# Laying rotated queries in DRAM once and reading them twice over, with a new order around the first sequence's stacks

## The chip, the core and the metric

The kernel runs on one core of one Trainium2 chip. The metric is the device time of one execution in microseconds (us). All engine names are those of the profile: PE is TensorE with PEld for its weight loads, DVE is VectorE, ACT is ScalarE, POOL is GpSimd, SP is SyncE. SP computes nothing here; it issues nearly all DMAs, one after the other, in the order in which the program lists them ("SPq" in the profile). 16 DMA engines move the data.

## What is computed

For each of 8 sequences x of 512 tokens and 256 features:

```
xn = layernorm(x)
q, k, v = xn @ in_proj_w.T, 16 heads of 16 features; q and k rotated (rope)
s = softmax(q k' / 4, keys j with 0 <= t - j < 250) v, then @ out_proj_w.T
h = relu([xn, -xn] @ +-1 weights) -> 1024; relu(h @ +-1 weights) -> 1024; -> 256
out = x + s * silu(h)
```

Everything is fp32. The +-1 weight matrices come as booleans.

## The kernel before, in words

**Splitting numbers in two.** A matmul reads its fp32 operands with fewer bits than they have. So q and k are split into a high part (hi) and a low part (lo), and a score is built as hi·hi + lo·lo + hi·lo + lo·hi. One head has 8 feature pairs x 2 places in the pair = 16 rows; the four products make 64 rows of contraction, and two heads fill 128 partitions. Such a 128-row operand is called a stack. A stack of k and one of q serve a pair of heads; a group g is four heads, so it has two pairs and needs four stacks. There are four groups in a sequence.

**How a stack is made.** `project` (L371) computes one half of q or k for all heads on PE into PSUM, DVE multiplies it with the rope tables (L397), `rotate` (L414) adds on POOL. `split_hi` (L431) rounds the high part on ACT into the tile `hi` and calls `to_dram`; `split_lo` (L437) subtracts on DVE and calls `to_dram` for the low part. `to_dram` (L420) writes each part to DRAM twice, by two DMAs of 512 KB: for k in the order hi, lo, hi, lo in a head's rows, for q in the order hi, lo, lo, hi, so that all four products meet when the 64 rows are contracted. `stack` (L444) then reads, for each pair and for k and q, 128 rows of 512 numbers (256 KB) from consecutive DRAM rows into an SBUF tile: four DMAs for a group, each out of the double-buffered pool `stacks` (bufs=2 for each of k0, q0, k1, q1).

**Attention.** A sequence has six steps (L702 to L721). `scores` (L735) does 12 matmuls for a step: first four of pair 0, then four of pair 1 (both with y = 0), then two each. Group 0 is used in steps 0 and 1, group 1 in 1 and 2, group 2 in 3 and 4, group 3 in 4 and 5. `exponentials` (L756) runs ACT over the score banks, `mask` (L781) clears on POOL, and the step after that multiplies with the values (`values`, L810). When a group is done, `keep` (L839) copies the PSUM bank `po` twice: for even groups into V (times a 0/1 column) and S by ACT, for odd groups by DVE.

**The order of the work.** `run` (L234) sorts pieces by a planner's time, in units in which one sequence takes 42, and emits them; each engine executes its instructions in that order. A piece may return followers with a delay; `project` gives `rotate`, `split_hi` (after `hi_after`) and `split_lo` (after `lo_after`), counted in the same units. `attention` (L869) places the steps among the matmuls of the feed-forward network and places the stack reads: in the first sequence (b = 0) groups 0 and 1 are read together at planner time 24.7 - 7.6 = 17.1; in later sequences group 0 is read before the sequence starts and group 1 just after it has started. The layernorm moments of sequence 1 go through DRAM as well: `lay_down` (L283) at 16.9 transposes on DVE and issues four small DMAs (L289), `load_xT` (L279) at 17.15 loads x transposed, and `lay_over` (L291) at 17.2 reads the moments back, spread over all partitions, in one DMA (L298, tile `of_all`). DVE then normalizes (L309), and PE projects k (L381, tile `ka_ps`).

**Division.** Sums of exponentials go through DRAM: `gather` (L913, tile `dsums`, DMAs of four rows), `pack` (L922, `sums`), `invert` (L929, `inv`), `unpack` (L942, `rows`). All are issued by SP, in line with the stack reads. Each next DMA of the chain waits on SP until the one before it has landed.

Of the kernel before, what the change touches and what calls it, by code (L numbers as in the profile page):

```python
# [11 lines left out]
F32 = mybir.dt.float32  # L12
# [4 lines left out]
ALU = mybir.AluOpType  # L17
# [17 lines left out]
def tile_attention_times_gated_ffn(  # L35
# [42 lines left out]
    nc = tc.nc  # L78
    P = 128
    B, T, E = x.shape  # L80
    H = HEADS
    D = E // H
# [19 lines left out]
    dram = ctx.enter_context(tc.tile_pool(name="dram", bufs=2, space=bass.MemoryType.DRAM))  # L102
# [4 lines left out]
    def bank(name):  # L107
        return ps_b.tile([P, T], F32, tag="b", name=name)
# [12 lines left out]
    first_half, second_half = s_sb[:, 3:4], s_sb[:, 4:5]  # L121
# [48 lines left out]
    rows = const.tile([P, T], F32, name="rows")  # L170
# [200 lines left out]
    def project(b, what, part, half=None):  # L371

        st = states[b]
        col = E * "qk".index(what) + P * "ab".index(part)
        if half == 1:
            ps = st.pop(part)
        else:
            ps = st[part] = bank(f"{what}{part}_ps_{b}")
        for cols in [slice(0, T)] if half is None else [ts(half, T // 2)]:
            for c in range(EC):  # L380
                nc.tensor.matmul(  # L381
                    ps[:, cols], wqkv_sb[:, c, ds(col, P)], st["xT"][:, c, cols],
                    start=(c == 0), stop=(c == EC - 1),
                )
        if half == 0:
            return

        m = turned.tile(
            [P, 2, T], F32, tag=f"m{part}", name=f"m_{what}{part}_{b}",
            bufs=2 if part == "a" else 1,  # L390
        )
        st[what, part] = m

        hi_after, lo_after = (4.0, 5.1) if b else (5.0, 6.2) if what == "k" else (4.6, 5.4)

        def times(i):
            nc.vector.tensor_tensor(  # L397
                m[:, i], ps, rope_sb[:, i if part == "a" else 1 - i], ALU.mult
            )

        def both():
            times(0)
            times(1)
            if part == "b":
                return [
                    (1.4, lambda: rotate(b, what)),
                    (hi_after, lambda: split_hi(b, what)),
                    (lo_after, lambda: split_lo(b, what)),
                ]


        return [(1.5 if b == 0 and what + part == "qb" else 0.0, both)]

    def rotate(b, what):  # L414
        st = states[b]
        m, n = st[what, "a"], st.pop((what, "b"))
        for i, op in enumerate((ALU.subtract, ALU.add)):
            nc.gpsimd.tensor_tensor(m[:, i], m[:, i], n[:, i], op)  # L418

    def to_dram(b, what, part, tile_):  # L420

        st = states[b]
        if part == 0:
            st["dram", what] = dram.tile([P, 8, T], F32, tag=what, name=f"d{what}_{b}")
        for turn in range(2):
            place = 2 * turn + (part ^ (turn if what == "q" else 0))
            nc.sync.dma_start(
                st["dram", what][:, ds(2 * place, 2), :], tile_.bitcast(F32)
            )

    def split_hi(b, what):  # L431
        st = states[b]
        hi = st["hi"] = turned.tile([P, 2, T], F32R, tag="hi", name=f"{what}h_{b}")
        nc.scalar.copy(hi, st[what, "a"])
        to_dram(b, what, 0, hi)

    def split_lo(b, what):  # L437
        st = states[b]
        m = st.pop((what, "a"))
        lo = m.bitcast(F32R)  # L440
        nc.vector.tensor_tensor(lo, m, st["hi"].bitcast(F32), ALU.subtract)
        to_dram(b, what, 1, lo)

    def stack(b, g):  # L444
        st = states[b]
        for pair in range(2):
            for what in "kq":
                t = stacks.tile([P, T], F32R, tag=f"{what}{pair}", name=f"{what}_{b}_{g}_{pair}")
                rows = st["dram", what][ds(32 * g + 16 * pair, 16)]
                nc.sync.dma_start(t.bitcast(F32), rows.rearrange("p n t -> (p n) t"))  # L450
                st[what, g, pair] = t

    def prepare(b, plain=False):
# [26 lines left out]
        for what in "kq":  # L480
            for n, part in enumerate("ab"):
                if b == 0 and what == "k" and not plain:

                    out += [
                        (-34.3 if n == 0 else -32.95, 0.87, lambda p=part: project(b, "k", p, 0)),
                        (at["k"] + dp * n, 0.87, lambda p=part: project(b, "k", p, 1)),
                    ]
                else:
                    out.append((
                        at[what] + dp * n, 1.75, lambda w=what, p=part: project(b, w, p),  # L490
                    ))
# [347 lines left out]
    def keep(b, g, po):  # L839

        st = states[b]
        odd = g % 2
        S = st["S", g] = outs.tile([P, T], F32, tag="S", name=f"S_{b}_{g}", bufs=3)
        if odd:
            V = st["V", g // 2]
            nc.vector.scalar_tensor_tensor(V, po, second_half, V, ALU.mult, ALU.add)
            nc.vector.tensor_copy(S, po)
        else:
            V = st["V", g // 2] = outs.tile(
                [P, T], F32, tag=f"V{g // 2}", name=f"V_{b}_{g}", bufs=2  # L850
            )
            nc.scalar.mul(V, po, first_half)
            nc.scalar.copy(S, po)

    def flush():
        if pending:
# [4 lines left out]
    def step(b, i):  # L861
        sc = scores(b, i)
        had = len(pending)
        more = flush() or []
        tiles, exps, rest = exponentials(b, i, sc)
        pending.append((rest, (b, i, tiles)))
        return [(-1.4 if had else 0.0, exps)] + more

    def attention(b, among):  # L869

        first, end = SEQ * b + (24.7 if b == 0 else 0.0), ends_at(b)
        inside = sorted((at, cost) for at, cost, _ in among if first <= at < end)
        whole = sum(cost for _, cost in inside)
        times, done = [], 0.0
        places = {}
        for at, cost in inside:
            if at in quick or b == 0 and at not in inner:
                places[at] = done
            done += cost
        for n in range(len(steps)):  # L880
            at = min(places, key=lambda at: abs(places[at] * len(steps) - whole * n))
            del places[at]
            times.append(at - 0.01)
        out = []
        for n in range(len(steps)):
            out.append((times[n], 2.5, lambda n=n: step(b, n)))
        for g in range(NG):

            at = times[used[g - 2][-1]] + 0.01 if g > 1 else first - (
                7.6 if b == 0 else 4.0 if b == 1 else 9.0  # L890
            )
            if b and g == 3:
                at += 5.0
            if b and g == 1:
                at = first + 0.01
            out.append((at, 0, lambda g=g: stack(b, g)))
        if b + 1 == B:
            out.append((end, 0.7, flush))
        return out

    def ends_at(b):
        return SEQ * b + (33.0 if b + 1 == B else SEQ)
# [158 lines left out]
    for b in range(B):  # L1061
# [4 lines left out]
        for t in range(NT):  # L1066
            if b + 1 < B:
                at = SEQ * b + 1.5 if b else 2.0
                everything.append((at + t, 0, lambda b=b, t=t: load_x(b + 1, t)))
        everything += divisions(b) + finish(b, b + 1 == B)  # L1070
    for b in range(B):
        everything += attention(b, everything)
# [54 lines left out]
    with tc.If(found < n_rows, label="general"):  # L1127
        for b in range(B):
            for t in range(NT):
                load_x(b, t)  # L1130
            run(prepare(b, plain=True))
            plain_ffn(b)
            for u in range(len(outputs(b))):
                run(finish_ffn(b, u, "at once"))
            for g in range(NG):
                stack(b, g)
                po = ps_o.tile([P, T], F32, tag="po", name=f"f_po_{b}_{g}")
                for t in range(NT):
                    for r in range(4):
                        shifted(b, g, t, r, po)  # L1140
                keep(b, g, po)
                if g % 2:
                    run(divisions(b, (g // 2,)))
            run(finish(b))
# [59 lines left out]
```

## Time and profile before

| | |
|---|---|
| runs | 598.86 us median of 3 (598.08 to 601.21) |
| the profiled execution | 598.20 us; its span from first to last instruction 596.5 us |
| granted TensorE clock in it | 0.999 |
| PE busy | 584.8 us, 98% of the span |
| DVE, ACT, POOL busy | 333.7, 303.0, 269.9 us |
| DMA | 92.24 MB, mean 155 GB/s; 38.30 MB written to and 53.22 MB read from DRAM (HBM) |
| queue q1 (SP's DMAs) | 47600 packets, 89.31 MB, 44.1% of the 16 engines' time |
| stack reads | 64 of k and 64 of q, 256 KB each |
| writes of q and k | 32 for each, 512 KB each |

The profile comes from one execution; 1.7 us of its time lie before its first and after its last instruction. A row of a timeline gives start and duration in us from the span's start, the engine, the source line, the operation, out<-in, and how many instructions were merged. For a DMA such a row is only the issue on SP; when the data is there is told by its landing events, of which each DMA engine that took part in a DMA sends one.

### The profile page before, as it was taken

Reading aid. Unit: us, or ns where it says so; the run is one execution under the profiler, and the core shown is the slowest. Engines: PE = TensorE matmul, PEld = TensorE weight load, DVE = VectorE, ACT = ScalarE, POOL = GpSimd, SP = SyncE. Lnnn points to the kernel's source line nnn. Section 1 sums busy time; section 2 is a strip of 40 time slices with the busy share of each in tenths; the row PEclk is TensorE's granted clock in tenths of the full one; section 3 lists DMA queues with packets and bytes.
Section 4 is the critical chain, followed back from the end, with each engine's and each line's share of the span. In section 5 each row is a group of like instructions: output and inputs, shape, how many; then the busy total and the mean of one; then the engine's idle time right before and its main releaser. Section 6 shows DMA issues by size and latency. Waiting matters only on the chain.

```text
span 596.5 us, 10410 instructions
## 1 busy us (share of the span) xinstructions
PE 584.8 (98%) x3788; PEld 364.7 (61%) x3788; DVE 333.7 (56%) x578; ACT 303.0 (51%) x571; POOL 269.9 (45%) x474
## 2 busy tenths in 40 slices
PE   7999999999999999999999999999999999999996
PEld 6655565655655556555566556665566555657785
DVE  6936335666346754478436684366744666427256
ACT  4747564545464545536454465544644645465422
POOL 2736533436334552445444355333652437435513
PEclk9999999999999999999999999999999999999999
DMA  9764844337432474415654075441673335441111
GB/s 277 283 234 143 294 152 127 108 141 250 146 117 98 170 240 133 147 65 223 208 165 154 2 293 189 130 142 65 238 228 113 107 135 208 158 143 43 35 28 53
DMA packets 50086, 92.24 MB, mean 155 GB/s; under 512 B 10992, under 2 KB 18672, under 8 KB 50032
## 3 DMA queue, kind: packets, MB, share of 16 engines
q1 hardware_dynamic: 47600, 89.31, 44.1%
q10 hardware_dynamic: 2432, 2.23, 1.2%
q8 instruction: 31, 0.51, 0.3%
q14 instruction: 23, 0.19, 0.1%
HBM read 53.22 MB, written 38.30 MB: 153 GB/s over the span
## 4 chain that ended last, share of the span: by engine, by line
PE 88%; DVE 3%; DMA 3%; ACT 2%; SPq 1%; POOL 1%; issue 1%; DVEq 0%; POOLq 0%; ACTq 0%
PE h_ps L511 44%; PE po L828 11%; PE z_ps L562 9%; PE sc L746 7%; PE v_ps L361 4%; PE att_ps L962 4%; PE ka_ps L381 2%; PE qb_ps L381 2%; PE qa_ps L381 2%; PE kb_ps L381 2%; DMA of_all<-d 1%; DMA dq<-m_qa 1%; PE warm L232 1%; SPq L450 1%; DMA dk<-kh 1%
## 5 line engine op out<-in xcount | busy, mean ns | idle before, releaser
L771 ACT ACTIVATE p<-sc 128x512 f32<-128x512 f32 (+2 forms) x288 | 150.2, 607 | 57.6 <-PE sc L746 57.4
L791 POOL TENSOR_SCALAR_AFFINE_SELECT p<-p 128x256 f32<-128x256 f32 (+1 forms) x224 | 104.8, 479 | 123.1 <-ACT p L771 105.4
L511 PE MATMUL h_ps<-h1l,w_sb 128*128 128x512 f32 (+1 forms) x576 | 145.3, 394 | 0.0
L511 PE MATMUL h_ps<-h1h,w_sb 128*128 128x512 f16 (+1 forms) x576 | 123.1, 356 | 0.0
L511 PEld LDWEIGHTS h_ps<-h1l,w_sb 128*128 128x128 f32 x576 | 100.4, 188 | 27.4 <-issue 5.7
L511 PEld LDWEIGHTS <-w_sb 128*128 128x128 f16 x704 | 61.3, 98 | 86.3 <-issue 41.5
L522 ACT ACTIVATE h2h<-h_ps 128x512 f16<-128x512 f32 (+1 forms) x72 | 39.6, 550 | 133.1 <-PE h_ps L511 133.1
L520 DVE SCALAR_TENSOR_TENSOR h2l<-h_ps,h2h 128x512 fp32r<-128x512 f32 (+1 forms) x72 | 44.8, 622 | 93.9 <-ACT h2h L522 93.4
L828 PE MATMUL po<-p,v_pad 128*32 128x378 f32 (+4 forms) x1152 | 71.5, 380 | 0.0
L520 DVE SCALAR_TENSOR_TENSOR h1l<-h_ps,h1h 128x512 fp32r<-128x512 f32 x64 | 43.2, 688 | 45.3 <-ACT h1h L522 45.1
L798 POOL TENSOR_SCALAR_AFFINE_SELECT p<-p 128x256 f32<-128x256 f32 x144 | 57.5, 399 | 0.3 <-POOL p L791 0.3
L746 PEld LDWEIGHTS sc<-q,k 64*128 64x128 f32 x576 | 41.9, 186 | 25.0 <-issue 15.1
L633 DVE RECIPROCAL den<-den 128x256 f32<-128x256 f32 (+1 forms) x32 | 52.4, 1641 | 3.7 <-ACT den L628 3.7
L746 PE MATMUL sc<-q,k 64*128 64x378 f32 (+4 forms) x576 | 52.2, 310 | 2.2 <-ACT p L771 1.2
L522 ACT ACTIVATE h1h<-h_ps 128x512 f16<-128x512 f32 x64 | 37.6, 603 | 30.0 <-PE h_ps L511 30.0
L511 PE MATMUL h_ps<-xl,w_sb 128*128 128x512 f32 x128 | 52.3, 489 | 0.0
L952 POOL TENSOR_TENSOR V<-V,R 128x512 f32<-128x512 f32 x16 | 21.2, 1327 | 52.4 <-DVE R L951 52.4
L828 PEld LDWEIGHTS po<-p,v_pad 128*32 128x32 f32 x1152 | 30.7, 109 | 21.2 <-issue 12.0
L991 POOL TENSOR_TENSOR gate<-gate,xr 128x512 f32<-128x512 f32 (+1 forms) x15 | 18.6, 1242 | 47.6 <-DVE gate L984 26.6
L418 POOL TENSOR_TENSOR m_qa<-m_qa,m_qb 128x512 f32<-128x512 f32 x16 | 21.1, 1343 | 38.5 <-DVE m_qb L397 38.5
L511 PE MATMUL h_ps<-xh,w_sb 128*128 128x512 f16 x128 | 38.5, 383 | 0.0
L562 PE MATMUL z_ps<-h2l,w_sb 128*128 128x512 f32 (+1 forms) x144 | 35.6, 389 | 0.0
(102 smaller groups left out, 656.9 us busy)
## 6 DMA issues: line engine op xcount, KB each, us to landing
k<-dk SPq DMA_DIRECT2D x64, 256.0 KB
q<-dq SPq DMA_DIRECT2D x64, 256.0 KB
dk<-kh SPq DMA_DIRECT2D x16, 512.0 KB
dk<-m_ka SPq DMA_DIRECT2D x16, 512.0 KB
dq<-qh SPq DMA_DIRECT2D x16, 512.0 KB
dq<-m_qa SPq DMA_DIRECT2D x16, 512.0 KB
x<-in_x_dram SPq DMA_DIRECT2D x30, 128.0 KB
xT<-in_x_t_dram SPq DMA_DIRECT2D x7, 512.0 KB
```

Source lines behind the costliest of these rows:

```text
L361: nc.tensor.matmul(v.rearrange("p n s d -> p (n s d)"), st["xT"][:, c, ts(t, P)], wqkv_sb[:, c, 2 * E :], start=(c == 0), stop=(c == EC - 1),)
L381: nc.tensor.matmul(ps[:, cols], wqkv_sb[:, c, ds(col, P)], st["xT"][:, c, cols], start=(c == 0), stop=(c == EC - 1),)
L511: nc.tensor.matmul(ph, weights(w, p, c, ts(f, P)), st[src + p][:, c, cols], start=(k == 0), stop=(k == n - 1),)
L520: nc.vector.scalar_tensor_tensor(lo, ph, 0.0, hi, ALU.max, ALU.subtract)
L522: high = lambda: nc.scalar.activation(hi, ph, AF.Relu)
L562: nc.tensor.matmul(pz, weights(w2, p, c, ts(f, P)), st["h2" + p][:, c, cols], start=(c == 0 and p == "h"), stop=(c == NF1 - 1 and p == "l"),)
L633: nc.vector.reciprocal(part, part)
L746: nc.tensor.matmul(sc[r + (4 if y else 2 * pair)][:, ds(at, n)], st["k", g, pair][row, ts(j, P)], st["q", g, pair][row, ds(j * P + first, n)],
L771: nc.scalar.activation(p, s_, AF.Exp, scale=D ** -0.5)
L791: nc.gpsimd.affine_select(out=block, in_=block, compare_op=ALU.is_ge, fill=0.0, base=0, pattern=[[0, heads], [1, P]], channel_multiplier=-1,)
L798: nc.gpsimd.affine_select(out=block, in_=block, compare_op=ALU.is_ge, fill=0.0, base=-1, pattern=[[0, heads], [-1, beyond]], channel_multi ...
L828: nc.tensor.matmul(po[32 * r : 32 * r + 32, ds(j * P + first, n)], v_columns(j, g, r), place(tiles_, r, y, off, n), start=(j == 0), stop=( ...
```

## The change

Three things change.

1. `to_dram` writes q once (one DMA for each part instead of two); k is still written twice, now itself with the two parts swapped in its second copy. The DRAM tile has the dimensions head, copy, feature pair, part, place, token. `stack` reads k as before. It reads q with two DMAs for each stack, one for each head: the head's 32 rows (64 KB) are the source, given twice over by a dimension of step 0 and size 2 ahead of the 32, and 64 partitions are the destination (128 KB).
2. In sequence 0, the stacks of group 0 are read at planner time 16.8, ahead of the moments (16.9), and those of group 1 at 17.0, behind them. In sequence 1 the high part of q is split 0.7 units earlier.
3. In sequence 0, `keep` of the even groups runs on DVE instead of ACT.

```
         hi_after, lo_after = (4.0, 5.1) if b else (5.0, 6.2) if what == "k" else (4.6, 5.4)
+        if b == 1 and what == "q":
+            hi_after = 3.3
...
         if part == 0:
-            st["dram", what] = dram.tile([P, 8, T], F32, tag=what, name=f"d{what}_{b}")
-        for turn in range(2):
-            place = 2 * turn + (part ^ (turn if what == "q" else 0))
+            n = 1 if what == "q" else 2
+            st["dram", what] = dram.tile(
+                [H, n, D // 2, 2, 2, T], F32, tag=what, name=f"d{what}_{b}"
+            )
+        d = st["dram", what]
+        for turn in range(d.shape[1]):
             nc.sync.dma_start(
-                st["dram", what][:, ds(2 * place, 2), :], tile_.bitcast(F32)
+                d[:, turn, :, part ^ turn].rearrange("h p i t -> h p (i t)"),
+                tile_.bitcast(F32).rearrange("p i t -> p (i t)"),
             )
...
-                rows = st["dram", what][ds(32 * g + 16 * pair, 16)]
-                nc.sync.dma_start(t.bitcast(F32), rows.rearrange("p n t -> (p n) t"))
+                of_heads = st["dram", what][ds(4 * g + 2 * pair, 2)]
+                rows = of_heads.rearrange("h r p a i t -> (h r p a i) t")
+                if what == "k":
+                    nc.sync.dma_start(t.bitcast(F32), rows)
+                else:
+                    for r in range(2):
+                        nc.sync.dma_start(
+                            t[ts(r, 64)].bitcast(F32),
+                            rows[ts(r, 32)].unsqueeze(0).broadcast_to([2, 32, T]),
+                        )
...
-            nc.scalar.mul(V, po, first_half)
-            nc.scalar.copy(S, po)
+            if b == 0:
+                nc.vector.tensor_scalar(V, po, first_half, None, ALU.mult)
+                nc.vector.tensor_copy(S, po)
+            else:
+                nc.scalar.mul(V, po, first_half)
+                nc.scalar.copy(S, po)
...
-                7.6 if b == 0 else 4.0 if b == 1 else 9.0
+                7.9 if b == 0 else 4.0 if b == 1 else 9.0
...
-            if b and g == 1:
-                at = first + 0.01
+            if g == 1:
+                at = first + 0.01 if b else at + 0.2
```

## The prediction

> **What bounds the kernel now.** First the page: PE is busy for 98% of the span, and 88% of the chain that ended last is PE. So I looked for what PE waits for, in the list of waits filtered to PE, the second fence (what waited, for whom, us in total, times, longest):
>
> ```profile
> PE 584.8 (98%) x3788; PEld 364.7 (61%) x3788; DVE 333.7 (56%) x578; ACT 303.0 (51%) x571; POOL 269.9 (45%) x474
> ...
> q1 hardware_dynamic: 47600, 89.31, 44.1%
> ```
>
> ```profile
> PE warm L232 <- POOL ident masks.py:199: 2.8, 1, 2.8
> PE sc L746 <- ACT p L771: 1.2, 1, 1.2
> PE sc L746 <- DMA q<-dq: 1.0, 1, 1.0
> ...
> PE ka_ps L381 <- DVE xT L309: 0.2, 1, 0.2
> ```
>
> The reader is to see how little is there. Outside the start and the end PE waits 2.36 us: 1.20 at 38 us, in the first step's scores; 0.19 at 47 us for the normalized x of sequence 1; 0.97 at 78 us for the first q stack of sequence 1. From 80 to 510 us no window shows a PE gap. The 1.20 is charged to ACT, but ACT's exponentials come after these scores; the landing events show the stacks of pair 1 landing at 37.9 and 39.2 us, and the PE resumes at 39.26. It is a DMA.
>
> So the change can win 2.4 us at most (0.4%), and the question is what it can lose. For that I read SP's timeline beside PE's, around the start of sequence 3 (start us, us, what was issued; the second fence is PE's first scores):
>
> ```profile
> 206.95 0.79 SPq L427 DMA_DIRECT2D dq<-qh  x2
> ...
> 209.26 1.06 SPq L427 DMA_DIRECT2D dq<-m_qa  x2
> 210.70 1.92 SPq L918 DMA_DIRECT2D dsums<-S  x2
> 215.03 0.32 SPq L926 DMA_DIRECT2D sums<-dsums  x1
> 215.45 0.38 SPq L450 DMA_DIRECT2D k<-dk  x1
> 215.93 0.37 SPq L450 DMA_DIRECT2D q<-dq  x1
> 216.39 0.38 SPq L450 DMA_DIRECT2D k<-dk  x1
> 216.82 0.42 SPq L450 DMA_DIRECT2D q<-dq  x1
> ...
> 223.23 1.07 SPq L945 DMA_DIRECT2D rows<-inv  x2
> ...
> 224.88 0.44 SPq L450 DMA_DIRECT2D k<-dk  x1
> ```
>
> ```profile
> 222.94 1.07 PE L746 MATMUL sc<-q,k 64*128 64x378 f32 x12
> ```
>
> The fourth stack lands at 221.73 (landing events) and PE wants it at 222.94 + 0.35 (after four matmuls of pair 0). The slack is 1.6 us, in every sequence: 293.84 against 294.99 in the next. Group 1's stacks land at 230.87 for 236.75: 5.9 us. Groups 2 and 3 have 12 to 16 us.
>
> **The q read, the part that decides.** In the trace a DMA is shared out by its outermost count: the 128-row DMAs leave 16 landing events, the eight-row `d<-moments` 9 and the four-row `dsums<-S` 5 (in the last two one is the issuer's). So four rows ran on four engines. The new source is [2, 32, 512], two copies outermost; the destination has 64 partitions. The bounds are 16 engines, like the 128-row reads, and two. I take two, by the four-row row, to which it is nearest.
>
> The Trainium skill, "DMA: Bandwidth & Descriptors", has this rule in its sections "Why a DMA increments its semaphore by 16 and not by 1" and "Rules for kernel authors": the slowest dimension of both sides sets the number of engines, and a leading zero-stride broadcast of c copies confines a DMA to c engines, the lowest-numbered ones. It speaks against the change; the rows with 5 and 9 events agree with it, and no run here shows a broadcast of two.
>
> Price on those two engines: a 2 KB packet takes 84 ns (median of the trace's 22272; in four quiet stack reads the first engine's landings follow at 0.67 us for 8 packets), or 96.5 ns by the queue line (0.441 x 16 x 596.5 us for 89.31 MB). I take 88. One q DMA then has 32 packets on each of the two: 2.8 us, where a whole stack took 0.7. A group's load, in issue order k0 q0 q0 k1 q1 q1: 0.7 + 5.6 + 0.7 + 5.6 = **12.6 us of the same two engines**, plus 1.9 us of latency (k alone lands 2.57 after issue, less 0.67). Before, the four landed 4.3 to 5.7 us after issue.
>
> **The start of each later sequence.** What helps: the dropped writes. Second `dq<-m_qa` landed at 214.74, the small `dsums` behind it at 214.97, and only then SP issued `sums` and the stacks. With one write of each part, m_qa issued at 209.26 lands at 211.9 (2.65 us, as an unqueued write at 198.20), the sums are through at 212.2, and k0 issues at 212.7: 2.75 us earlier. Last landing 212.7 + 1.9 + 12.6 = 227.2; PE wants it at 223.3: **3.9 us of waiting**. Then the second: `inv<-sums`, issued behind the stacks, also has rows on those engines and lands about 228.9; SP waits for it with `rows`, then the output, then group 1, which so issues at 230.4 instead of 224.88. It lands at 244.9; PE wants it at 236.75 + 3.9 + 0.35 = 241.0: **3.9 more**. Group 2 issues when step 1 is done (about 245.5) and lands near 260; it is wanted at 263.4. Group 3 and `of_all` fit in the same way, barely. So 7.8 us a sequence; for sequences 2 to 7, 6 x 7.8 = 46.8. In sequence 7 step 1 follows step 0 after 10.2 us instead of 13.8: 3.6 more.
>
> **Sequences 0 and 1**, same arithmetic. The early order lets group 0's q issue at 30.3, when its one write has landed; k0 has been read before, so 11.9 us are left: 30.3 + 1.9 + 11.9 = 44.1 instead of 39.2 wanted at 38.0: 6.1, of which 1.2 was there: +4.9. Group 1 behind it: 56.7, wanted at 43.66 + 4.9 + 0.35 = 48.9: +7.8. The moments, now behind group 0 on SP, cross the same engines (eight rows), and `of_all` with xT queues behind group 1: about 60; normalized (2.75 us on DVE) it is wanted at 46.2 + 12.7: +3.3. Group 3's load follows group 2's and the k writes: about 88.3 against 82.4: +6. Sequence 1's q is on hand about 93.6; last landing 107.4 against 99.9: 7.5, less the 0.97 there: +6.5. Together 28.5.
>
> **The rest costs nothing.** Even groups on DVE: two instructions of 0.75 and 0.68 us (its odd-group rows) at 52 and 74 us, where DVE then waits 4.0 and 4.7 us; without that cover 1.4 us each. ACT gains 1.3 us that ends no PE wait. The earlier `split_hi` puts the cast (1.04 us) at 65.9, when POOL is done, ahead of `h2h` instead of behind it: 0.76 us earlier, while `h2h` and DVE's subtraction behind it may come 0.5 later; queued behind is no PE bank that is short. Bounds -1 to +1. SP issues 8 more reads and 2 fewer writes a sequence, 6 x 0.43 = 2.6 us; it waited 18.2 us in one go for `kh` alone. The k order is free.
>
> **The clock.** Four matmuls of one shape (`xnT_ps`) took 1.11 us at 6.96 and 0.60 at 9.51, so PE starts slow; its granted clock is still 1.00 for 4.5 us after its last matmul and then 0.51. Waits of 6 us or more may bring the slow state back; no row shows it in the middle. From 0 to 2.8 us (half of the 5.6 from first matmul to full speed) after each of the four long waits: 0 to 11, I take 4.
>
> The skill's page "TensorE: Matmul & The Clock Gate", Part 1, gives half rate after an idle window of about 3.4 us; by that the 3.9 us waits too could cost up to 1.7 each, an estimate of 20 us more. The tail (4.5 us at 1.00) speaks against so short a limit.
>
> **Sum:** 46.8 + 3.6 + 28.5 + 4 = 83 on the profiled execution's 598.2: **681 us**, +14%. That execution lies 0.7 below the median of the runs, which changes nothing here.
>
> **Rivals.**
> - *Forecast*, two engines at 84 to 92 ns, 630 to 725 us: chance 0.67. At the low end the chains in sequences 0 and 1 partly hide and packets take 84 (group 12.1 us, waits 3.3).
> - *The two engines saturate*, 725 to 800 us: 0.20. Per 72 us sequence they carry 16 x 2.8 = 45 us of q and 44.1% of 72, less the old q reads (5.6) and dropped writes (2.6), = 24: 69 of 72 already. At 96.5 ns a load is 13.9 us; the waits grow by 1.3 each and a third one appears at `ka_ps` since `of_all` queues too: about 725, and steep beyond. For it: a few packets in each load take 0.6 to 0.9 us.
> - *Not slower*: 0.10. The read is spread over 16 engines after all (the copies are folded into the 64 partitions or split finer). It decides from about 8 engines on: a load is then as short as now, the 1.20 and the 0.97 go, and `of_all`, a few issues later, holds PE at `ka_ps` for about what was won: 595.8 to 598.5, about 597.2.
> - *Four engines*: 0.03. Load 7 us, landing at 221.6: no wait in later sequences; sequence 0 about +8: 606.
>
> **Numbers.** The range 630 to 770 takes in the forecast and most of saturation and leaves out about 0.2. A difference of 0.5% is about what a measurement of this kernel tells from none. Faster by more would need over 3 us where 2.36 are on offer: 0.02; within 0.5%: 0.08; slower: 0.90.
>
> **What would show it.** Right: `q<-dq` x128 with few landing events each; PE's waits led by `sc <- DMA q<-dq` (or k) with over 50 us, two for each sequence; written bytes down by 8 MB; SP's waits for `inv` and `dsums` up. Wrong: 16 engines in each q DMA and PE at 98%; or two engines, but the waits at `ka_ps` or at the clock instead of the scores.

## The result and the profile after

The changed kernel takes 732.1 us at the median of 6 runs (729.85 to 732.53) against 598.93 us, the median of 6 runs of the kernel before: a ratio of 1.2213, with a 95% interval of 1.2187 to 1.2238. The profiled execution took 731.19 us, its span 729.5 us. The time lies inside the range of the prediction, 51 us above its point, in the case that was called saturation.

Three parts of the page after (busy time; DRAM traffic; the chain that ended last), and one row of its DMA issues:

```profile
PE 634.5 (87%) x3788; PEld 384.9 (53%) x3788; DVE 341.4 (47%) x582; ACT 302.9 (42%) x567; POOL 268.6 (37%) x474
...
q1 hardware_dynamic: 44528, 80.92, 35.0%
...
HBM read 53.22 MB, written 29.91 MB: 114 GB/s over the span
...
PE 43%; DMA 41%; DVE 6%; SPq 5%; ACT 2%; issue 2%; POOL 1%; POOLq 0%; DVEq 0%; ACTq 0%
...
q<-dq SPq DMA_DIRECT2D x128, 128.0 KB
```

Fewer bytes are moved and the DMA engines are, on average, less busy than before (35.0% for 44.1%), yet DMA now holds 41% of the chain. An average over 16 engines hides that two of them carry all q reads: of the landing events, each q read leaves 3 (two engines and the issuer), each k read 16. A q read, now half the size, lands 10.3 us after its issue at the median (4.6 before). That it is the same two engines each time shows in the DMAs that use all 16: at the start of sequence 3, pair 1's k was issued at 271.39, and 14 of its 16 landing events came by 274.41, the last two at 279.12 and 279.90. Of `inv<-sums`, only 16 KB, issued at 277.12, 14 came by 278.89 and the last two at 286.00 and 286.64.

PE's waits in the kernel after (who waited for whom, us, times, longest):

```profile
PE sc L760 <- DMA q<-dq: 67.5, 31, 3.4
PE ka_ps L381 <- DVE h2l L534: 16.0, 6, 4.4
PE warm L232 <- POOL ident masks.py:199: 2.8, 1, 2.8
PE sc L760 <- DVE h1l L534: 1.7, 1, 1.7
```

PE's idle time grew by 83.3 us (95.0 for 11.7), its busy time by 49.7 us with the same 3788 instructions. The second part is the clock. Its records show 18 stretches at half clock, each 3.4 us or a multiple of it, 105.8 us in all ahead of the tail; half of that is 52.9 us. Before there was none. The timeline and two windows around step 1 of sequence 3 show how it comes (timeline: start, us, line, instruction, idle before it and its releaser; windows: stretch, length, busy us of PE, PEld, DVE, ACT, POOL, granted clock, DMA share, GB/s):

```profile
301.42 0.78 PE L760 MATMUL sc<-q,k 64*128 64x378 f32 x7
303.76 0.61 PE L760 MATMUL sc<-q,k 64*128 64x128 f32 x5 [1.56 <-DMA q<-dq]
304.31 2.54 PE L842 MATMUL po<-p,v_pad 128*32 128x378 f32 x24
```

```profile
301.00:304.00 3.00, 1.44 (x14) 0.87 (x13) 0.75 (x1) 1.56 (x3) 0.77 (x3) 1.00 0.13 48
304.00:308.20 4.20, 4.20 (x33) 1.99 (x31) 0.00 (x0) 0.59 (x1) 1.48 (x4) 0.59 0.38 77
```

A wait of 1.56 us was enough: the values' 24 matmuls then took 2.54 us instead of 1.49.

By sequences, from step 0 to step 0 (the last to the end of the span), in us:

| sequence | 0 | 1 | 2 | 3 | 4 | 5 | 6 | 7 |
|---|---|---|---|---|---|---|---|---|
| before | 40.0 | 73.3 | 72.0 | 72.0 | 72.0 | 72.0 | 72.0 | 85.4 |
| after | 67.6 | 88.3 | 86.4 | 87.4 | 86.9 | 88.5 | 84.1 | 102.8 |

So a later sequence lost 12 to 17 us where 7.8 were forecast (11.4 for the last). SP's timeline at the same place in the work, the start of sequence 3:

```profile
266.00 0.32 SPq L432 DMA_DIRECT2D dq<-m_qa  x1
266.37 1.18 SPq L936 DMA_DIRECT2D dsums<-S  x2
269.28 0.32 SPq L944 DMA_DIRECT2D sums<-dsums  x1
269.71 0.37 SPq L458 DMA_DIRECT2D k<-dk  x1
270.17 1.13 SPq L461 DMA_DIRECT2D q<-dq  x2
271.39 0.38 SPq L458 DMA_DIRECT2D k<-dk  x1
271.82 1.20 SPq L461 DMA_DIRECT2D q<-dq  x2
...
286.65 1.08 SPq L963 DMA_DIRECT2D rows<-inv  x2
287.82 0.39 SPq L1010 DMA_DIRECT2D out_dram<-gate  x1
288.31 0.38 SPq L458 DMA_DIRECT2D k<-dk  x1
...
304.86 0.33 SPq L944 DMA_DIRECT2D sums<-dsums  x1
305.29 0.38 SPq L458 DMA_DIRECT2D k<-dk  x1
...
321.44 1.08 SPq L963 DMA_DIRECT2D rows<-inv  x2
323.35 0.35 SPq L298 DMA_DIRECT2D of_all<-d  x1
```

The one write of each part helps as foreseen (`sums` follows m_qa after 3.3 us instead of 5.8). Then everything with a share on the two engines queues there: the last q lands at 285.15, 15.4 us after k0's issue; `inv<-sums`, issued at 277.12, lands at 286.64; SP has been waiting for it with `rows` and can only then issue group 1's stacks. The same comes twice more. Group 1's last q lands at 303.72, and `dsums`, for which SP waits with `sums`, at 304.85; group 2, issued at 305.29, lands at 321.19, and the next `inv` at 321.38. Only then come `rows` and `of_all`. So three loads of 15.4, 15.4 and 15.9 us stand one behind the other ahead of the moments.

### The profile page after: what moved, and what is told of

It is laid out like the page before. It is cut to its first block, busy times and chain, and to the rows that moved or that the text cites. A ratio compares the mean times of both kernels' runs of the same rounds, so it can differ in the third digit from the quotient of the medians.

```text
span 729.5 us, 10471 instructions
## 1 busy us (share of the span) xinstructions
PE 634.5 (87%) x3788; PEld 384.9 (53%) x3788; DVE 341.4 (47%) x582; ACT 302.9 (42%) x567; POOL 268.6 (37%) x474
## 4 chain that ended last, share of the span: by engine, by line
PE 43%; DMA 41%; DVE 6%; SPq 5%; ACT 2%; issue 2%; POOL 1%; POOLq 0%; DVEq 0%; ACTq 0%
DMA q<-dq 24%; PE h_ps L525 19%; PE po L842 7%; DMA k<-dk 6%; PE sc L760 4%; DMA d<-moments 4%; SPq L461 3%; PE ka_ps L381 3%; PE z_ps L576 3%; DMA dq<-m_qa 2%; DVE xT L309 2%; PE kb_ps L381 2%; PE att_ps L980 2%; PE qa_ps L381 2%; DMA sums<-dsums 2%
## 5 line engine op out<-in xcount | busy, mean ns | idle before, releaser
L525 PE MATMUL h_ps<-h1l,w_sb 128*128 128x512 f32 (+1 forms) x576 | 148.9, 401 | 0.0
L760 PE MATMUL sc<-q,k 64*128 64x378 f32 (+4 forms) x576 | 67.7, 338 | 69.2 <-DMA q<-dq 67.5
L525 PE MATMUL h_ps<-h1h,w_sb 128*128 128x512 f16 (+1 forms) x576 | 125.2, 361 | 0.0
L525 PEld LDWEIGHTS h_ps<-h1l,w_sb 128*128 128x128 f32 x576 | 102.8, 192 | 30.0 <-issue 7.7
L525 PEld LDWEIGHTS <-w_sb 128*128 128x128 f16 x704 | 61.8, 99 | 91.2 <-issue 47.2
L760 PEld LDWEIGHTS sc<-q,k 64*128 64x128 f32 x576 | 50.2, 203 | 98.3 <-issue 59.7
L842 PE MATMUL po<-p,v_pad 128*32 128x378 f32 (+4 forms) x1152 | 89.9, 457 | 0.0
L536 ACT ACTIVATE h1h<-h_ps 128x512 f16<-128x512 f32 x64 | 37.5, 602 | 63.5 <-PE h_ps L525 63.5
L525 PE MATMUL h_ps<-xl,w_sb 128*128 128x512 f32 x128 | 53.6, 499 | 0.0
L842 PEld LDWEIGHTS po<-p,v_pad 128*32 128x32 f32 x1152 | 36.8, 128 | 30.4 <-issue 23.2
L970 POOL TENSOR_TENSOR V<-V,R 128x512 f32<-128x512 f32 x16 | 20.4, 1278 | 74.1 <-DVE R L969 74.1
L525 PE MATMUL h_ps<-xh,w_sb 128*128 128x512 f16 x128 | 40.4, 399 | 0.0
L381 PE MATMUL ka_ps<-xT,wqkv_sb 128*128 128x512 f32 (+1 forms) x36 | 22.6, 764 | 16.9 <-DVE h2l L534 16.0
L309 DVE TENSOR_TENSOR xT<-xT,of_all 128x512 f32<-128x512 f32 x28 | 18.7, 690 | 39.3 <-DMA of_all<-d 28.2
```

The lines of the kernel that those rows point to most:

```text
L309: nc.vector.tensor_tensor(xT, xT, st["of_all"][:, i], op)
L381: nc.tensor.matmul(ps[:, cols], wqkv_sb[:, c, ds(col, P)], st["xT"][:, c, cols], start=(c == 0), stop=(c == EC - 1),)
L525: nc.tensor.matmul(ph, weights(w, p, c, ts(f, P)), st[src + p][:, c, cols], start=(k == 0), stop=(k == n - 1),)
L536: high = lambda: nc.scalar.activation(hi, ph, AF.Relu)
L760: nc.tensor.matmul(sc[r + (4 if y else 2 * pair)][:, ds(at, n)], st["k", g, pair][row, ts(j, P)], st["q", g, pair][row, ds(j * P + first, n)],
L842: nc.tensor.matmul(po[32 * r : 32 * r + 32, ds(j * P + first, n)], v_columns(j, g, r), place(tiles_, r, y, off, n), start=(j == 0), stop=( ...
```

## The experiments

Theory 1: the source's outermost count of two confines each q read to two engines, and all of the loss follows. Theory 2, the rival: it is the number of DMAs, or reading a DRAM row twice, or another part of the change. Within theory 1 there are two readings of where the 133 us are: theory A adds the waits (83) and the slow clock (50); theory B says that a loop of transfers over the two engines, closed by the moments that PE's projection of k needs, sets the length of a sequence, and slow matmuls beside it cost nothing.

**All 16 engines, more DMAs (e1_q_spread).**

```
-                    for r in range(2):
-                        nc.sync.dma_start(t[ts(r, 64)], rows[ts(r, 32)].unsqueeze(0).broadcast_to([2, 32, T]))
+                    for r in range(4):
+                        nc.sync.dma_start(t[ts(r, 32)], rows[ts(r // 2, 32)])
```

> Only the q read of the changed kernel is altered: each stack of q is read by four DMAs of 32 rows to 32 partitions instead of two with the copies outermost. Bytes, order and all else stay; SP issues even more DMAs (q<-dq x256). Theory 1 (each copy-outermost read runs on two engines; everything else follows from that): 16 engines, no wait at the scores in later sequences, clock back near 1.00, 596 to 604 us. Rival theory 2 (the number of DMAs that SP issues, or reading one DRAM row twice, is what costs): not below 700 us.

603.81 us, ratio 1.0082 (1.0058 to 1.0106), clock 0.989. With twice as many q DMAs 128 us of the 133 are gone, so neither their number nor the second reading of a row is the cause, nor the new layout in DRAM, which this run keeps. In the profiled execution (607.33 us, the slowest of five) most of the rest has a place: a wait of 3.4 us for the normalized x at the start, one of 1.0 us for q at 86 us, and with the two waits half-clock stretches of 6.8 and 3.4 us.

```profile
PE ka_ps L381 <- DVE xT L309: 3.4, 1, 3.4
...
PE sc L757 <- DMA q<-dq: 1.0, 1, 1.0
```

**The copies innermost (e2_q_inner).** The rows of a stack are put in the order head, pair, part, place, copy.

```
-                [H, n, D // 2, 2, 2, T], F32, ...
+                [H, D // 2, 2, 2, n, T], F32, ...
...
-                d[:, turn, :, part ^ turn].rearrange("h p i t -> h p (i t)"),
+                d[:, :, part ^ turn, :, turn].rearrange("h p i t -> (h p) i t"),
...
+                    rows = of_heads.rearrange("h p a i r t -> (h p a i) r t")
+                    nc.sync.dma_start(t.bitcast(F32), rows.broadcast_to([64, 2, T]))
```

> The changed kernel with another order of rows in a stack: the two copies of a row lie next to each other, so that q is still written once, but a whole stack is read by one DMA whose source is [64 rows, 2 copies, 512] with the rows outermost; k is laid in DRAM to match, in pieces of 2 KB. Theory 1: 16 engines, 595.8 to 598.5 us, that is 0 to 0.5% faster than before, with 8 MB fewer written. Theory 2 (reading a DRAM row twice over costs by itself): over 640 us.

596.41 us, ratio 0.9949 (0.9934 to 0.9964): faster than the kernel before, and 136 us below the change that wanted the same. All of PE's waits that the prediction counted, at 38, 47 and 78 us, are gone. These are all of PE's waits in this kernel:

```profile
PE warm L232 <- POOL ident masks.py:199: 2.8, 1, 2.8
PE sc L757 <- DVE h2l L531: 0.8, 1, 0.8
PE ka_ps L381 <- ACT xT L344: 0.5, 1, 0.5
PE z_ps L573 <- ACT h2h L533: 0.4, 1, 0.4
PE h_ps L522 <- ACT p L782: 0.2, 1, 0.2
```

**Only the order of the dimensions (e9_two_inner).** The layout of e2_q_inner, but again two DMAs of 64 partitions for each stack:

```
+                    for r in range(2):
+                        nc.sync.dma_start(t[ts(r, 64)], rows[ts(r, 32)].broadcast_to([32, 2, T]))
```

> As in the changed kernel, q is read by two DMAs of 128 KB for each stack, one for each head, 32 DRAM rows twice over into 64 partitions; only the order of the source's dimensions differs: [32 rows, 2 copies, 512] instead of [2 copies, 32 rows, 512] (k laid out to match). Theory 1: 16 landing events for each DMA and one by the issuer at most, no wait in later sequences, 596 to 600 us. If anything in the read but the outermost count (two DMAs of 64 partitions for a stack, a row read twice) carries the loss: over 620 us.

599.03 us, ratio 0.9976 (0.9954 to 0.9998), 16 landing events for each q read; the four of the first load of sequence 3 land 2.9 to 4.2 us after issue (6.2 to 12.6 in the changed kernel). This is the tightest pair: same number, size and destinations of the q reads, same source rows twice over. What is different is which dimension leads, and 133 us; the order of k's rows goes with it, but e1_q_spread, which has k as in the changed kernel, doesn't have the loss.

**The parts alone (e3_only_q, e4_no_q).** Part 1 put into the kernel before, and the changed kernel with part 1 taken out.

```
 e3_only_q: before.py with to_dram and stack of the change
 e4_no_q:   the changed kernel with to_dram and stack of before
```

> The kernel before with the new q write and read alone (copies outermost), without the new order in sequence 0, the earlier split and the VectorE copies. Theory 1: 725 to 740 us, the whole of the change's loss. A rival by which the new order around sequence 0 or the copies on VectorE carry part of it: under 715 us.

> The changed kernel without its new q write and read: the new order of group 0's stacks, moments and group 1's stacks in sequence 0, the earlier split of q's high part in sequence 1 and the even groups' copies on VectorE remain. Theory 1: no loss, 596.5 to 599 us; the 1.2 us wait in the first step goes, and the wait for the normalized x takes most of it. A rival by which the order costs: over 601 us.

736.56 us, ratio 1.2289 (1.2258 to 1.2319), and 598.39 us, ratio 0.9986 (0.9972 to 0.9999). Part 1 carries the whole loss, and since e1_q_spread keeps its write, it is the q read. The other parts are worth 0.1%: in the trace of e4_no_q the wait of the first step is gone, 1.3 us ahead of `ka_ps` have taken its place, and the 0.9 us for q at sequence 1 remain. Beside the confined read they win some 4 us (736.56 against 732.1).

**Half of the confinement (e6_half).** Pair 1's q by 32-row reads, pair 0's as in the change.

```
+                        if pair:
+                            for c in range(2):
+                                nc.sync.dma_start(t[ts(2 * r + c, 32)], rows[ts(r, 32)])
+                            continue
```

> The changed kernel with pair 1's q read by four 32-row DMAs (16 engines) and pair 0's as in the change (two engines): half of the confined bytes. Theory 1 with deadlines (a load matters only where it lands after PE wants it; a group's load is now about 8 us of the two engines, within the 10 us of later sequences): no wait at the scores in sequences 2 to 7, 600 to 615 us. Rival (the loss goes with the confined bytes): half of the 133 us, 655 to 675 us.

637.18 us, ratio 1.0642 (1.0610 to 1.0675): between the two numbers, so neither fits as stated. The trace, of the fastest of four executions, tells why. From sequence 2 to 6 the distance of step 0 to step 0 is 73.3 to 74.1 us, 1.3 to 2.0 over before, with one wait of 0.3 to 0.8 us each: half the confined bytes cost about a tenth of the 15 us, as a deadline would have it. But sequence 0 alone is 17 us longer (step 0 to step 0 57.2), and its start had no slack to begin with; sequence 7, whose step 1 follows sooner, is 6.7 us longer. Theory 1's deadlines hold for sequences 2 to 6 to within these 2 us, and my number for the start was wrong.

**Work put into the waits of steps 0 and 1 (e5_warm_steps).**

```
+                        n_warm = {(0, 0): 20, (0, 1): 18}.get((i, r), 0) if (j, y) == (0, 0) else (
+                            13 if i == 1 and (j, y, r) == (3, 0, 1) else 0
+                        )
+                        for _ in range(n_warm if b and pair == 1 else 0):
+                            nc.tensor.matmul(sc[r + 2][:, ds(at, P)], ident, ident, start=True, stop=True, ...)
```

> The changed kernel with idle matmuls (identity times identity, overwritten by the scores that follow in the same bank) put where PE waits in steps 0 and 1 of sequences 1 to 7: 20 and 18 ahead of pair 1's first two scores in step 0, 13 ahead of its last in step 1, some 2.3, 2.1 and 1.5 us of work. Theory A (waits and slow clock add: of the 133 us about 83 are waits and 50 are matmuls at half clock, and keeping PE busy in the waits saves most of the second part): 685 to 700 us. Theory B (a loop of transfers over the two engines, from group 0's load to the moments that ka_ps needs, sets the length of a sequence; the half-clock stretches after steps 0 and 1 lie beside that loop): the clock goes up to 0.96 or more, the waits grow by what the matmuls gain, 722 to 735 us.

726.71 us, ratio 1.2137 (1.2100 to 1.2174), clock 0.973. An idle matmul is two instructions of 118 ns, so the work was twice what I had reckoned. Its timeline in sequence 3 shows PE without a gap where it waited:

```profile
277.40 4.73 PE L764 MATMUL sc<-ident 128*128 128x128 f32 x40
282.06 0.44 PE L768 MATMUL sc<-q,k 64*128 64x378 f32 x1
282.43 4.29 PE L764 MATMUL sc<-ident 128*128 128x128 f32 x36
286.64 0.79 PE L768 MATMUL sc<-q,k 64*128 64x378 f32 x7
...
300.88 3.17 PE L764 MATMUL sc<-ident 128*128 128x128 f32 x26
```

That is 12.2 us of useless work a sequence, 85 us in seven, and half-clock time fell from 105.8 to 37.5 us, which gives 34 us of matmul time back. The idle matmuls ran past the end of the waits, so that in sequence 3 the last scores of step 0 began 20.1 us after k0's issue instead of 16.5; even so `of_all` landed 57.2 us after it (57.6 in the changed kernel) and `ka_ps` began at 60.7 (61.0). The total moved by 5 us. PE's time around steps 0 and 1 is not what sets the length, fast or slow; theory A falls. (The waits for q at the scores are 19.5 us here instead of 67.5, since the idle matmuls fill them.)

**Work put ahead of ka_ps (e8_warm_ka).** The same kind of matmuls, 20 of them, ahead of k's first projection.

```
+        for _ in range(20 if b and what + part == "ka" else 0):
+            nc.tensor.matmul(ps[:, :P], ident, ident, start=True, stop=True, ...)
```

> The changed kernel with 20 idle matmuls (2.3 us) ahead of the first projection of k in sequences 1 to 7, where PE waits 2 to 4.4 us for the normalized x. Theory B (this wait is in the loop, and so are the 3.4 us at half clock that follow it): 8 to 12 us faster than the changed kernel, 720 to 724 us. Theory A gives about the same here, 718 to 726; a rival by which the clock matters nowhere: 731 to 735 us.

758.59 us, ratio 1.2642 (1.2601 to 1.2682): 26 us slower than the change, outside all three expectations. Its timeline shows why it could not do what I wanted:

```profile
337.81 1.90 PE L527 MATMUL h_ps<-h1h,w_sb 128*128 128x512 f16 x8
342.98 7.59 PE L380 MATMUL ka_ps<-ident 128*128 128x128 f32 x40 [3.27 <-DVE h2l L536]
350.40 1.88 PE L383 MATMUL ka_ps<-xT,wqkv_sb 128*128 128x512 f32 x4
```

The wait stands ahead of the idle matmuls, not behind them. What PE waits for is not x but the PSUM bank: it becomes free when DVE has done `h2l`, and that stands on DVE behind the normalization, which waits for `of_all`. So the matmuls came on top, 7.6 us here at mostly half clock, 4.6 to 7.6 in each sequence and 40 us in seven, of which the total shows 26. As a test of the clock it failed; as a test of place it is the counterpart of e5_warm_steps. The same kind of work is nearly free at steps 0 and 1 and costs here. The three traces, from k0's issue in sequences 1 to 6, in us:

| | changed kernel | e5_warm_steps | e8_warm_ka |
|---|---|---|---|
| last scores of step 0 begin | 16.4 to 18.8 | 19.4 to 21.8 | 16.3 to 19.3 |
| `of_all` lands | 56.1 to 58.6 | 56.4 to 58.0 | 56.3 to 59.4 |
| k's first projection begins | 59.5 to 62.1 | 60.1 to 61.8 | 64.7 to 69.0 |
| from there to the next k0 | 24.7 to 27.4 | 24.6 to 25.6 | 24.4 to 25.1 |

Work on PE at steps 0 and 1 does not move `of_all`, work ahead of k's projection moves the next sequence: this is the loop of theory B. One part of theory B is too strong. The half-clock matmuls behind `ka_ps` lie in the loop, and the last row is where e5_warm_steps won: 6.5 us over the six sequences.

**What the small parts are worth (e7_inner_act, e10_inner_only).** e2_q_inner with the even groups' copies on ACT, and the kernel before with the q write and read of e2_q_inner alone.

> The kernel with the copies innermost (e2_q_inner), but the even groups' copies of sequence 0 on ScalarE again. If the 0.8 us wait of scores for VectorE at 57 us is due to the copies: it goes, and the time is 0.5 to 0.8 us under e2_q_inner's. If VectorE's copies cost nothing, as predicted: within 0.5 us of it.

> The kernel before with q written once and read with the copies innermost, one DMA for a stack, and nothing of the new order in sequence 0, the earlier split and the VectorE copies. Theory 1 with the small parts near zero: 596 to 598 us, since the shorter writes alone take away the waits for q at 38 and 78 us. If the new order is needed for the gain seen with the copies innermost: 598 us or more.

596.33 us, ratio 0.9946 (0.9924 to 0.9968), with a wait of 0.7 us for `h2l` still there: the copies on DVE cost nothing and win nothing. 598.40 us, ratio 0.9978 (0.9962 to 0.9994), with waits of 0.9 us for q in the first step (at 40.8 us) and 0.2 us for x: the shorter writes alone take the wait of sequence 1 away, not that of the first step. For that one the new order is needed, as e4_no_q shows from the other side. The new order with the earlier split seems to be worth another 0.3% on top; the intervals of the two ratios just touch, so this is not settled.

## Why the prediction was right, and where it was off

The direction and its cause, q reads on two engines, were right. That the time lies inside the range is in part luck. The forecast case (630 to 725 us) had the right price of a packet and missed the time. The saturation case (725 to 800 us, chance 0.20) had the time and the third wait, but not for its reason, packets of 96.5 ns on two engines with no time left: in sequence 3 the four loads took 63 of 87 us. Of the 51 us that were missing, 40 lie in sequences 2 to 7 (90.7 lost, 50.4 forecast) and 14 in sequences 0 and 1; against these stand the 4 us that the sum had for the clock, which the sequences' losses contain. And the sign named for "right", waits led by the scores' wait for q, was there with 67.5 us, though the experiments show that these waits are not what sets the length.

- **What could be won** (2.4 us): right. e2_q_inner, which does all the change set out to do, has a span 2.0 us shorter; its runs are 2.8 us faster at the median.
- **Two engines**: right, read off the four- and eight-row DMAs and borne out by three landing events for each q read. The Trainium skill's rule on a leading zero-stride broadcast ("DMA: Bandwidth & Descriptors", "Rules for kernel authors") holds here for the number of engines, 3 events for two copies outermost, 16 with 32 or 64 rows outermost. That they are the lowest-numbered ones, no run shows.
- **Price of a read**: about right. The two q reads of a pair land 2.7 us apart (median of 64 pairs), 84 ns a packet, where I took 2.8. The load of a group took 15.4 to 16.4 us in sequence 3 instead of 14.5. In the first load the first confined read landed 4.1 us behind k0 where its packets account for 2.7; in the next two it was 3.4 and 2.5. Why they differ is open. The prediction's "4.3 to 5.7 us" for the four reads of a load before leaves out the quicker ones; all stack reads before took 2.5 to 5.7.
- **The sum for the later sequences**, 7.8 us each: this is the step that failed. The waits at the scores were there (in sequence 3 4.7 us in step 0 and 1.6 in step 1), but "Group 3 and `of_all` fit in the same way, barely" did not hold. Group 2 landed 51.5 us after k0's issue where the prediction's times give 47.3, and behind it `of_all` waited 2.2 us more on SP, for `inv` and `rows`, and took 4.0 us to land, for which the sum had no term. It was issued 53.6 us after k0 (34.3 before), landed at 327.3, and with it the rest of DVE's queue was late. DVE's timeline there:

```profile
323.96 0.74 DVE L969 STREAM_SHUFFLE R<-rows 128x512 f32<-128x512 f32 x1
327.33 2.75 DVE L309 TENSOR_TENSOR xT<-xT,of_all 128x512 f32<-128x512 f32 x4 [2.63 <-DMA k<-dk]
329.99 0.68 DVE L534 SCALAR_TENSOR_TENSOR h2l<-h_ps,h2h 128x512 fp32r<-128x512 f32 x1
```

  The view puts DVE's wait down to `k<-dk`, but the last landing event of `of_all` came at 327.30, that of this k at 328.01. `ka_ps` resumed 0.1 us behind this `h2l`, at 330.73. From k0's issue to there are 61.0 us; from there to the next k0 (356.99) 26.3, where before took 26.9. So the loop has a part over the two engines that grew by 16 (44.9 before) and a part that starts with PE and did not grow. The prediction had this wait in its saturation case, "a third one appears at `ka_ps`", to which I had given 0.20.
- **The clock**, 4 us: far too small as a count of slow time (52.9 us lost), and yet most of that is no term of the sum, since slow matmuls beside the loop do not lengthen it; those behind `ka_ps` do. I had weighed the Trainium skill's page "TensorE: Matmul & The Clock Gate", Part 1 (half rate after an idle window of about 3.4 us), against the kernel's tail and believed the tail. The trace after sides with the page on the length, stretches of 3.4, 6.8 and 10.2 us, and goes further than its idle window: a wait of 1.56 us sufficed.
- **Sequences 0 and 1**, 28.5 us together: 27.6 and 15.0 measured. Sequence 0 was forecast at 22 up to the next step 0. The rest of sequence 1, its own loop, I had left out.
- **The rest costs nothing**: right for the copies and the order (e4_no_q, e7_inner_act). "The k order is free" was not quite: a k write in the new shape takes SP 0.57 us instead of 0.32 and lands 4.1 us after issue instead of 2.6 when nothing is ahead of it. Nobody waits for it in the later sequences.

## What to carry to other kernels

Look at the outermost dimension of every DMA before anything else: a copy or broadcast count placed there decides on how many engines the transfer runs (here 3 landing events instead of 16), and a mean DMA share of 35% says nothing about the two for which everything waits. The same data with the rows outermost and the copies inside went from 22% slower to 0.5% faster. And where PE waits and runs slowly at once, don't add the two up: put work into the wait, and see at which place it costs.

## What the runs showed of the hardware

- A wait of 1.0 to 1.6 us can already be followed by 3.4 us at half clock (e1_q_spread: 0.98 us; changed kernel: 1.56 us), though waits of the same size went by without it (0.97 and 1.20 us before). In the changed kernel all slow stretches ahead of the tail but the first, 10.2 us, are 3.4 or 6.8 us long.
- A 128-row DRAM write given as 16 x 8 rows landed 1.5 us later than the same bytes given as 128 rows, with 16 landing events in both (k's high part, nothing ahead of it: 4.1 us for 2.6, in every sequence).
- A DMA over all 16 engines was as late as the two busy ones among them: `inv<-sums`, 16 KB, had 14 landing events 1.8 us after its issue and the last two, behind the q reads, after 9.5 us (1.4 to 1.6 in the kernel before, with nothing ahead of it).
